# Combining the first expert layer and dispatching the second inside attention's steps, with heads spread through DRAM and packed loads

## The chip, the cores and the metric

The kernel runs on one core of one Trainium2 chip. TensorE (PE in the profile) does matrix products and transposes into PSUM; VectorE (DVE), ScalarE (ACT) and GpSimd (POOL) work on what stands there or in SBUF; SyncE (SP) and POOL issue the DMAs. The metric is the device time of one execution in microseconds. The kernel before has a median of 851.75 us over three runs, from 846.43 to 854.3.

## The reference

`x` is 8 sequences of 256 tokens with 128 features each, all in float32. Six blocks follow one another, each added to `x`:

```python
x = x + 0.5 * ffn(layernorm(x))          # mixture of experts, weights L0_ffn
x = x + attn(layernorm(x))               # 16 heads of 8
x = x + 0.5 * ffn(layernorm(x))          # the same mixture of experts again
x = x + 0.5 * channel_mix(layernorm(x))  # token shift, relu^2, sigmoid gate
x = x + gated_conv(layernorm(x))         # a long convolution by a Fourier transform
x = x + 0.5 * channel_mix(layernorm(x))

def ffn(s):                               # 2048 tokens
    h = rmsnorm(s @ W_in.T, in_norm_w)
    logits = h @ Wr.T                     # 8 experts
    idx = top_k(logits + expert_bias, 2)
    gates = softmax(logits at idx)        # 0 elsewhere
    out = sum over e of gates[:, e] * rmsnorm((silu(h @ Wg[e].T) * (h @ Wu[e].T)) @ Wd[e].T, enorm_w[e])
    return rmsnorm(out, out_norm_w) @ W_out.T
```

Attention is plain softmax attention within a sequence, with scale 8 ** -0.5.

## The kernel before

**Tiling.** The 2048 tokens are four chunks (`NCH`) of 512, each held as `xs[c]`, 128 partitions x 4 rows (`TPC`) x 128. Two sequences make a chunk. Everything up to the second expert layer stands in a hand-written order: PE, DVE, ACT and SP run their instructions in the order of the program (`manual_schedule`); only POOL's order is chosen by the scheduler.

**Expert layer, `moe_ffn(f, ...)`, f = 0 and 1.** `dispatch(f, c, mp)` gives four steps per chunk: `product` (four transposes of x into PSUM bank "sa", mean and variance on DVE, four products with `win_r`, squares on ACT), `normed` (a root on ACT, the scaled rows `hrow`, the logits), `choice` (13 small DVE operations for the top two, then PE's `prank` and DVE's `at_row`, `pos`, `posi`: the place of each row in its expert's region), and `rows` (eight indirect DMAs on POOL, L433, which scatter the rows to `hs` in DRAM). `stagger` (one step of each chunk in turn) interleaves the four chunks. `table` computes from the counts which expert and which rows each of 23 tiles of 256 rows takes. `experts` runs these tiles: SP fetches rows `hst_f` and the expert's weights `w_f` (832 KB) three tiles ahead, PE does gate, up and down, ACT and DVE the silu and the product, and POOL scatters the results to `y2` in DRAM (L568). `combine(f, c, ...)` has four steps: `fetch` (SP, two rows per token), `add` (a reciprocal root of 8 numbers per partition on POOL, L610, then eight DVE operations), `turned` (four transposes, squares on ACT, another root on POOL, L634) and `out_` (four products with `wout_o`, four DVE additions to x). In stage 0, all four chunks are combined before attention begins; in stage 1 all four are dispatched after attention has ended.

**Start.** About 28 small loads on SP, with the four chunks of x among the first ten, and eight DMAs that fill the row buffer `hs` with zeros (L117), 516 KB each. POOL clears the constant lanes of q, k, v and m meanwhile (L683, L684, L979).

**Attention.** 32 steps s = (sequence b, head group g of four heads), then eight more for what is left over. In step s, PE does `scores(s, 0)`, `turn_top(s - 1)`, `scores(s, 1)`, the step's extras, `weights(s - 1, 0)`, `average(s - 2)`, `weights(s - 1, 1)`; DVE does `qa` for step s - 1 (L799), `top(s, 0)`, the extras, `top(s, 1)` (L787); ACT does the two exponentials (L818) and every other step `keep`. The extras are listed by step: `turn_back`, `turn_heads` and `out_heads` of each sequence at 4b+6 to 4b+9 (`out_heads` adds to x), the parts of the filter's decay at steps 2, 4 and 6, and the projection of chunk c at 8c-7 (`norm_rows`), 8c-5 (`turn_rows`), 8c-4 and 8c-3 (`to_heads` for q and k) and 8c-2 (`values`). Chunk 0's projection stands before step 0. All extras share the PSUM bank "sa", one at a time, with the transposed maxima of `turn_top`. `norm_rows` takes mean and variance on DVE and the rest on POOL (L705 to L709). `to_heads` copies the product to SBUF, and then SP issues 16 DMAs of 16 KB, which spread the heads over partitions (L730).

After the second expert layer come `channel_mix`, `gated_conv` and `channel_mix`; they are scheduled, and not touched.

Of the kernel before, what the change touches and what calls it, by code (L numbers as in the profile page):

```python
# [10 lines left out]
F32 = mybir.dt.float32  # L11
# [5 lines left out]
P = 128  # L17
B, S, D = 8, 256, 128
NCH = 4
# [18 lines left out]
FILL = 8  # L38
# [5 lines left out]
def macaron_kernel(ctx: ExitStack, tc: tile.TileContext, a: dict, out: bass.AP):  # L44
# [42 lines left out]
    def load(name, shape, src=None, eng=None):  # L87
        t = const.tile(shape, F32, tag=name, name=name)
        (eng or nc.sync).dma_start(t, a[name] if src is None else src)
        return t  # L90

    def load_col(name):
        return load(name, [P, 1], a[name].rearrange("(p o) -> p o", o=1))

    load_x(0)
    win = load("win", [P, D])
    inw = load_col("inw")
    wr_t = load("wr_t", [P, E])
    load_x(1)
    eb = load("eb", [P, E], a["eb"].partition_broadcast(P))  # L100
    tabc = load("tabc", [P, 2 * E * E + 2 * NT * E + NT + 2 + 2 * E])
    tri = load("tri", [P, P])
    load_x(2)
    load_x(3)
    tokid = const.tile([P, NCH * TPC, 2], I32, tag="tokid", name="tokid")
    nc.sync.dma_start(tokid, a["tokid"])
# [3 lines left out]
    nc.vector.memset(zero, 0.0)  # L110


    hs = tc.dram_tile([HS_ROWS, ROW], F32, name="hs")
    region = hs[1 : 1 + E * REGION, :].rearrange("(e c p r) w -> e c p (r w)", e=E, c=2, r=8 * FILL)
    for e in range(E):
        some = zero[ts(e, P // E), :].unsqueeze(1).to_broadcast([P // E, 8, FILL * ROW])
        nc.sync.dma_start(region[e, 0].rearrange("p (i w) -> p i w", i=8), some)  # L117

    rpe_in = load("rpe_in", [P, FEAT], a["rpe_in"].partition_broadcast(P), eng=nc.sync)
    rpe_g = load("rpe_g", [P, LAYERS, FEAT], a["rpe_g"].partition_broadcast(P), eng=nc.sync)  # L120
    rpe_b = load("rpe_b", [P, LAYERS, FEAT], a["rpe_b"].partition_broadcast(P), eng=nc.sync)
    rpe_hid = load("rpe_hid", [FEAT, LAYERS, FEAT], a["rpe_hid"].rearrange("l i o -> i l o"), eng=nc.sync)
    rpe_out = load("rpe_out", [FEAT, D], eng=nc.sync)
    decay = load("decay", [P, D], a["decay"].partition_broadcast(P), eng=nc.sync)

    csm = load("csm", [P, 3])
    idx_col, onehot = csm[:, 0:2], csm[:, 2:3]
    onw = load_col("onw")
    wout_t = load("wout_t", [P, D])

    dft = load("dft", [P, 2, 512], a["dft"].rearrange("(i p) f -> p i f", p=P))
    idft = load("idft", [P, 4, S], a["idft"].rearrange("(q p) m -> p q m", p=P))

    wq_t = load("wq_t", [P, D])
    wk_t = load("wk_t", [P, D])
    wv_t = load("wv_t", [P, D])
    wo_t = load("wo_t", [P, D])
    rw_r = load("rw_r", [P, D])
    rw_k = load("rw_k", [P, D])
    rw_v = load("rw_v", [P, D])  # L140
    mu_r = load_col("mu_r")
    mu_k = load_col("mu_k")
    w_uv = load("w_uv", [P, 2 * D])
    w_go = load("w_go", [P, D])

    om_r = const.tile([P, 1], F32, tag="om_r", name="om_r")
    om_k = const.tile([P, 1], F32, tag="om_k", name="om_k")
    for dst, src in ((om_r, mu_r), (om_k, mu_k)):
        nc.vector.tensor_scalar(dst, src, -1.0, 1.0, ALU.mult, ALU.add)
# [170 lines left out]
    o += 2 * NT * E  # L320
    tid = tabc[:, o : o + NT]
    slot = tabc[:, o + NT : o + NT + 2]
    base = tabc[:, o + NT + 2 : o + NT + 2 + E]
    order = tabc[:, o + NT + 2 + E : o + NT + 2 + 2 * E]
# [6 lines left out]
    def dispatch(f, c, mp):  # L331
# [4 lines left out]
        def product():  # L336
# [16 lines left out]
            for t in range(TPC):  # L353
                nc.tensor.matmul(
                    st["pp"][:, t // 2, t % 2, :], xt[:, ts(t, P)], win_r, start=True, stop=True
                )
# [147 lines left out]
    def experts(f, tab, far, y2, mp, pieces):  # L504
# [74 lines left out]
        for t in range(3):  # L579
            fetch(t)  # L580
# [509 lines left out]
```

## Time and profile before

| | us |
|---|---|
| median of three runs (lowest, highest) | 851.75 (846.43, 854.3) |
| the profiled execution, its time | 851.69 |
| its span in the trace | 849.8 |
| start to first gate of stage 0 | 83.6 |
| experts, stage 0 | 83.6 to 217.2 |
| combination of four chunks, projection of chunk 0 | 217 to 292.5 |
| attention from the first `qa` to the last `out_heads` | 292.5 to 500.5 |
| dispatch of four chunks, table, first rows | 500.5 to 565.5 |
| experts, stage 1 | 565.5 to 695 |
| combination, channel mix, convolution, channel mix | 695 to 849.8 |

Mean granted TensorE clock 0.821 of full; PE busy 624.0 us (73%), DVE 393.1 (46%), ACT 260.7 (31%), POOL 251.2 (30%).

How to read it: the busy digits of the time slices and the stretches' table tell where an engine is full and where none is; a timeline line gives start, duration, engine, line of the kernel, operation, what it writes and reads, how often, and in brackets how long the engine had been idle and what ended that. `PEclk` is the granted clock of TensorE, 1.00 or 0.50 here. An average over the span says little, since the stages have different limits.

### The profile page before, as it was taken

What the parts mean: (1) busy time and instruction counts of PE and PEld (TensorE: products, weight loads), DVE (VectorE), ACT (ScalarE), POOL (GpSimd) and SP (SyncE); (2) the same over time, 40 slices, a digit from 0 to 9 for tenths busy, and PEclk for the clock granted to TensorE, in tenths of its full rate; (3) what the DMA queues carried; (4) which work ended last, traced back from release to release, by engine and by line L of the source; (5) the groups of instructions that cost most, each with busy time, mean ns of one, the idle gap of its engine ahead of it and who ended that gap; (6) DMA issues with size and microseconds to landing.
All of it is one profiled execution on the core that took longest, in us unless ns stands there. A gap on an engine that the chain in (4) does not pass through costs nothing. (4 is left out here: it accounts for less than half of the span.)

```text
span 849.8 us, 11683 instructions
## 1 busy us (share of the span) xinstructions
PE 624.0 (73%) x4019; PEld 478.3 (56%) x4019; DVE 393.1 (46%) x1017; ACT 260.7 (31%) x613; POOL 251.2 (30%) x250
## 2 busy tenths in 40 slices
PE   2520999999344599999999965249999963467974
PEld 2520889899232355656556535239999952344563
DVE  4660445444241243645545515614444434784684
ACT  3310232233221152444444443102323321446132
POOL 4276233333332010200200004722333333360353
PEclk9555999999755587999999975559999995598988
DMA  8723656664200001000010000155666603000001
GB/s 165 168 95 119 194 180 199 198 183 135 74 26 10 16 6 20 2 10 18 2 25 1 2 1 31 50 205 159 204 207 195 192 29 101 1 1 0 1 0 50
DMA packets 44619, 69.57 MB, mean 82 GB/s; under 512 B 7883, under 2 KB 34162, under 8 KB 44560
## 3 DMA queue, kind: packets, MB, share of 16 engines
q1 hardware_dynamic: 39568, 60.34, 24.8%
q0 software_dynamic: 4992, 8.48, 2.9%
q8 instruction: 32, 0.52, 0.2%
q14 instruction: 27, 0.22, 0.1%
HBM read 52.96 MB, written 15.58 MB: 81 GB/s over the span
## 5 line engine op out<-in xcount | busy, mean ns | idle before, releaser
L568 POOL DMA_INDIRECT y<-yrow_f,idx_f x92 | 90.1, 980 | 171.8 <-issue 166.2
L433 POOL DMA_INDIRECT hs<-hrow,posi_f x64 | 61.7, 964 | 153.6 <-DVE ri_f L369 108.6
L818 ACT ACTIVATE es<-ps 128x1024 f32<-128x1024 f32 x64 | 65.4, 1024 | 102.4 <-PE ps L810 102.4
L530 PE MATMUL pg_f<-ht_f,w_f 128*128 128x256 f32 x368 | 90.8, 391 | 5.0 <-DMA w_f<-in_wall_dram 5.0
L550 PE MATMUL py_f<-w_f,hg_f 128*128 128x128 f32 x736 | 90.2, 276 | 2.4 <-DVE yrow_f L561 2.4
L787 DVE TENSOR_REDUCE m<-pm 128x4 f32<-128x1024 f32 x64 | 77.2, 1216 | 31.4 <-PE pm L774 31.4
L774 PE MATMUL pm<-k,q 32*128 32x256 f32 x512 | 81.5, 439 | 13.8 <-DMA k<-kc 11.7
L550 PEld LDWEIGHTS py_f<-w_f,hg_f 128*128 128x128 f32 x736 | 88.6, 192 | 4.9 <-DVE yrow_f L561 2.7
L539 PE MATMUL pu_f<-ht_f,w_f 128*128 128x256 f32 x368 | 87.9, 382 | 0.0
L543 DVE TENSOR_TENSOR hg_f<-pu_f,sg_f 128x1024 f32<-128x1024 f32 x46 | 56.4, 1225 | 62.9 <-PE pu_f L539 62.9
L532 ACT ACTIVATE sg_f<-pg_f 128x1024 f32<-128x1024 f32 x46 | 47.1, 1024 | 117.3 <-PE pg_f L530 117.3
L810 PE MATMUL ps<-qa,k 32*128 32x256 f32 x512 | 76.5, 421 | 0.0
L530 PEld LDWEIGHTS pg_f<-ht_f,w_f 128*128 128x128 f32 x368 | 68.7, 197 | 13.7 <-issue 5.8
L539 PEld LDWEIGHTS pu_f<-ht_f,w_f 128*128 128x128 f32 x368 | 67.3, 193 | 7.4
L774 PEld LDWEIGHTS pm<-k,q 32*128 32x128 f32 x512 | 48.2, 204 | 26.0 <-DMA k<-kc 14.2
L560 ACT ACTIVATE ysq_f<-py_f 128x128 f32<-128x128 f32 x92 | 24.6, 273 | 122.9 <-PE py_f L550 117.6
L810 PEld LDWEIGHTS ps<-qa,k 32*128 32x128 f32 x512 | 46.3, 195 | 24.8 <-issue 16.2
L524 DVE TENSOR_SCALAR ht_f<-pht_f,inw 128x256 f32<-128x256 f32 x46 | 22.3, 484 | 67.4 <-PE pht_f L522 67.4
L799 DVE TENSOR_TENSOR qa<-pmt,q 128x256 f32<-128x256 f32 x32 | 13.6, 425 | 85.6 <-PE pmt L793 85.6
L522 PE MATMUL pht_f<-ident,hst_f 128*128 128x128 f32 x92 | 18.7, 287 | 40.6 <-DMA hst_f<-hs 40.6
L561 DVE TENSOR_TENSOR yrow_f<-py_f,w_f 128x256 f32<-128x256 f32 x46 | 19.6, 426 | 53.5 <-ACT ysq_f L560 53.5
L625 PE MATMUL pan_f<-ident,acc_f 128*128 128x128 f32 x32 | 9.4, 448 | 46.4 <-DVE acc_f L616 46.4
(244 smaller groups left out, 927.5 us busy)
## 6 DMA issues: line engine op xcount, KB each, us to landing
w_f<-in_wall_dram SPq DMA_DIRECT2D x46, 832.0 KB
hst_f<-hs SPq DMA_DIRECT2D x46, 129.0 KB
hs<-zero SPq DMA_DIRECT2D x8, 516.0 KB
y_f<-y SPq DMA_DIRECT2D x16, 258.0 KB
y<-yrow_f,idx_f POOLq DMA_INDIRECT x92, 4.5
x<-in_x_dram SPq DMA_DIRECT2D x4, 256.0 KB
hs<-hrow,posi_f POOLq DMA_INDIRECT x64, 2.4
q<-qc SPq DMA_DIRECT2D x64, 16.0 KB
```

The costliest lines, as they stand in the source:

```text
L433: ins = nc.gpsimd.indirect_dma_start(out=hs, out_offset=bass.IndirectOffsetOnAxis(ap=st["posi"][:, t, k : k + 1], axis=0), in_=hrows[c][:, ...
L530: nc.tensor.matmul(pg[:, k, :], w[t][:, ts(k, P)], ht[t], start=True, stop=True)
L532: nc.scalar.activation(sg, pg, AF.Silu)
L539: nc.tensor.matmul(pu[:, k, :], w[t][:, DFF + k * P : DFF + k * P + P], ht[t], start=True, stop=True)
L543: nc.vector.tensor_mul(hg[t], pu, sg)
L550: nc.tensor.matmul(py[:, s, :], hg[t][:, k, ts(s, P)], w[t][:, 2 * DFF + k * D : 2 * DFF + k * D + D], start=(k == 0), stop=(k == NFC - 1),)
L560: nc.scalar.activation(sq[:, s], py[:, s], AF.Square, accum_out=yrow[:, s, D : D + 1])
L568: ins = nc.gpsimd.indirect_dma_start(out=y2, out_offset=bass.IndirectOffsetOnAxis(ap=idx[:, s : s + 1], axis=0), in_=yrow[:, s, :], in_off ...
L774: nc.tensor.matmul(sc[:, jj, i, :], qs[c][r, g, col + i * P : col + (i + 1) * P], ks[c][r, g, col : col + S], start=True, stop=True,)
L787: nc.vector.tensor_reduce(m, sc, AX.X, ALU.max, negate=True)
L810: nc.tensor.matmul(sc[:, jj, i, :], ks[c][r, g, col + i * P : col + (i + 1) * P], tops[s][r, :], start=True, stop=True,)
L818: nc.scalar.activation(es, sc, AF.Exp, scale=scale)
```

## The change

1. *Order.* `moe_ffn` is taken apart. Stage 0's dispatch and experts run as before; `combined` then yields the steps of each chunk's combination (`add` together with the fetch of the chunk after next, `turned`, `out_`). Chunk 0's steps run before attention; chunk c's (c = 1 to 3) are extras of steps 8c-8 to 8c-6. The dispatch of stage 1 for chunk c is extras of steps 8c+14 to 8c+20, so chunks 0 and 1 lie within the 32 steps, chunk 2 has its last five steps after them, and chunk 3 all seven. The loop has 45 steps, not 40.
2. *Dispatch* has seven steps (`turned`, `product` twice, `normed`, `choice`, `places`, `rows`), goes through one bank at a time, and copies the product to SBUF (`u`). For f = 1 the root is POOL's, not ACT's.
3. *Projection*: `norm_rows` normalises on DVE, with only the root on POOL; it stands at 8c-5, `turn_rows` and the first `to_heads` share 8c-4, then 8c-3 and 8c-2. `to_heads` writes q and k of a chunk to DRAM in one DMA of 512 KB and reads them back, spread, in four of 128 KB.
4. *Loads*: five packs in place of the small loads; chunks 2 and 3 of x are loaded behind the zeros, which are written in pieces of half the size (`FILL` 4). ACT does a first Sqrt early. The constant lanes are cleared on POOL beside the first ten expert tiles. The weights of the first three tiles are fetched ahead of their rows; `yrow` has two buffers, not three.

The core of the diff:

```diff
-FILL = 8
+FILL = 4
...
     load_x(0)
+    win, wr_t, inw, eb, tri, slot, base, order, tokid = pack(
+        "pack1", [D, E, 1, E, P, 2, E, E, NCH * TPC * 2]
+    )
     load_x(1)
...
-        nc.sync.dma_start(region[e, 0].rearrange("p (i w) -> p i w", i=8), some)
+        nc.sync.dma_start(region[e, 0].rearrange("p (i w) -> p i w", i=16), some)
+    load_x(2)
+    load_x(3)
...
+        def product(i):
+            pp = bank(f"pin_{n}_{i}", "sa" if f else None)[:, 0 : 2 * (D + E)]
...
+            u = st["u"][:, 2 * i : 2 * i + 2]
+            nc.scalar.copy(u, pp)
...
+            if f == 0:
+                nc.scalar.activation(ri, ri, AF.Sqrt)
+                nc.vector.reciprocal(ri, ri)
+            else:
+                nc.gpsimd.tensor_tensor(ri, ri, mhalf.to_broadcast([P, TPC]), ALU.pow)
...
-        return product, normed, choice, rows
+        return turned, partial(product, 0), partial(product, 1), normed, choice, places, rows
...
         for t in range(3):
-            fetch(t)
+            fetch_weights(t)
+        for t in range(3):
+            fetch_rows(t)
...
-                nc.gpsimd.tensor_scalar(rs, mv[:, :, 1], LN_EPS, None, ALU.add)
+                nc.vector.tensor_scalar(rs, mv[:, :, 1], LN_EPS, None, ALU.add)
                 nc.gpsimd.tensor_tensor(rs, rs, mhalf.to_broadcast([P, TPC]), ALU.pow)
...
-                    nc.gpsimd.tensor_scalar(
+                    nc.vector.tensor_scalar(
...
-                for j in range(4):
-                    for g in range(4):
-                        r = 32 * j + HD * g
-                        nc.sync.dma_start(dst[32 * j : 32 * j + HD, g, :], t[r : r + HD, :])
+                if i == 1:
+                    there = tc.dram_tile([P, 2, CT], F32, name=f"heads{c}")
+                    nc.sync.dma_start(there, qkc[c])
+                    back = there.rearrange("(j g d) i s -> j d i g s", j=4, g=4)
+                    for j in range(4):
+                        nc.sync.dma_start(qks[c % 2][32 * j : 32 * j + HD], back[j])
...
+            for c in range(NCH):
+                project = [
+                    partial(norm_rows, c),
+                    partial(turn_rows, c),
+                    partial(to_heads, c, 0),
+                    partial(to_heads, c, 1),
+                    partial(values, c),
+                ]
+                if c == 0:
+                    for step in (*before[0], *project):
+                        step()
+                else:
+                    for i, step in enumerate(before[c]):
+                        extra[8 * c - 8 + i].append(step)
+                    for i, step in zip((-5, -4, -4, -3, -2), project):
+                        extra[8 * c + i].append(step)
+                for i, step in enumerate(after[c]):
+                    extra[8 * c + 14 + i].append(step)
...
+    def combined(f, gates, y2, gp):
+        chunks = [combine(f, c, gates, y2, gp) for c in range(NCH)]
+        for chunk in chunks[:2]:
+            chunk[0]()
+        ahead = [chunk[0] for chunk in chunks[2:]] + [lambda: None] * 2
+        return [(both(add, fetch), *rest) for fetch, (_, add, *rest) in zip(ahead, chunks)]
...
+            stagger([dispatch(0, c, gp) for c in range(NCH)])
+            gates = run_experts(0, y2s[0], gp, [both(*two) for two in zip(early, idle)])
+            mixed = combined(0, gates, y2s[0], gp)
+            attention(mixed, [dispatch(1, c, gp) for c in range(NCH)])
+            gates = run_experts(1, y2s[1], gp, [])
+            stagger(combined(1, gates, y2s[1], gp))
```

## The prediction

> **What bounds the kernel now.** I read the time slices first, then busy time by stretch, then the order of instructions around each seam, and last the order on VectorE inside attention. From the page, busy tenths in 40 slices of 21.2 us:
>
> ```profile
> PE   2520999999344599999999965249999963467974
> DVE  4660445444241243645545515614444434784684
> POOL 4276233333332010200200004722333333360353
> PEclk9555999999755587999999975559999995598988
> ```
>
> PE is full in the two expert stages and in attention. Between them lie two valleys with half of PE's clock: slices 11-14 (combining stage 0, projecting heads) and 24-26 (dispatch of stage 1). The stretches, columns PE, PEld, DVE, ACT, POOL, granted clock, DMA share, GB/s:
>
> ```profile
> 221.80:257.60 35.80, 13.00 (x48) 10.04 (x48) 13.73 (x61) 7.03 (x36) 10.50 (x8) 0.50 0.23 59
> ...
> 313.94:317.35 3.41, 1.66 (x20) 0.80 (x12) 0.59 (x2) 3.37 (x6) 0.00 (x0) 1.00 0.13 24
> ...
> 441.00:488.00 47.00, 47.00 (x470) 29.05 (x466) 27.11 (x38) 20.07 (x24) 0.00 (x0) 1.00 0.02 4
> 500.50:565.40 64.90, 23.07 (x92) 19.83 (x92) 28.73 (x157) 16.26 (x58) 30.81 (x32) 0.50 0.17 52
> ```
>
> In the valleys no engine is half busy: they are chains of waits. In 441-488 PE is never idle. So work taken out of a valley shortens it fully, and what it costs inside attention is what PE is made to do and to wait for.
>
> **The change part by part.** All sums start from the profiled execution: span 849.8 us, its time 851.69, 1.9 more; the median 851.75 is the same within 0.1 us.
>
> *Start.* The input of chunks 2 and 3 is now queued behind the eight transfers that zero the row buffer. These moved 4.2 MB at some 180 GB/s (stretch 6.0-33.6) and ended near 33.5. The hand order puts `turned(3)` ahead of chunk 0's `normed`, `choice` and `places` on PE, ACT and DVE, so chunk 0's first scatter waits for x3: about 32.7, then some 9.5 us of chain (positions came 10 us apart per chunk, at 27.6 and 37.7, and that round holds the same steps) and 0.9 to the scatter: 43.1 against 36.50. The 32 scatters keep their pace of 1.26 us. Weights fetched before the table's rows save some of the 2.3 us wait for `w_f` ahead of the first gate; I take 1.8. Together +4.8; below, -2 (the wait goes and x3 is early), above, +10 (zeros in pieces of half the size are slower). Clearing constants beside the experts adds some 13 us to POOL in ten tiles of 5.46 us whose scatters take 2 us each, and the output rows lose their third buffer: both are hidden by the 3.4 us that POOL has free per tile; without that cover, 0 to +5. The early Sqrt on ACT costs nothing before the first x lands.
>
> *Before attention.* Here is the seam, in the order of the trace:
>
> ```profile
> 226.47 0.17 DVE L609 TENSOR_SCALAR cf_f<-y_f 128x8 f32<-128x8 f32 x1 [6.37 <-DMA y_f<-y]
> 226.73 1.67 POOL L610 TENSOR_TENSOR cf_f<-cf_f,mhalf 128x8 f32<-128x8 f32 x1 [5.18 <-DVE cf_f L609]
> ...
> 256.44 1.13 DVE L643 SCALAR_TENSOR_TENSOR x<-pout_f,ori_f,x 128x128 f32<-128x128 f32 x4 [1.12 <-POOL ori_f L634]
> ...
> 278.30 10.65 SPq L730 DMA_DIRECT2D k<-kc  x16
> ...
> 292.50 0.42 DVE L799 TENSOR_TENSOR qa<-pmt,q 128x256 f32<-128x256 f32 x1 [0.84 <-PE pmt L793]
> ```
>
> Only chunk 0 is now combined here. Alone, it has x at 235.4 (sums 230.56, transposes, squares and POOL's root to 234.2, 1.1 on DVE) where all four took until 257.57: -22.2. The normalised rows go from POOL's 3.12 us to four of DVE's operations near 0.2 us: -2.3. So `kc` is ready at 245.45, not 269.98. The heads then took 18.3 us (269.98 to the last scores that waited for `k`, at 288.33), 32 issues of some 0.68 us on SP's queue, as the line at 278.30 shows for sixteen. Now one write of 512 KB is followed by four reads of 128 KB: a 258 KB transfer took 3.8 us here (222.68 to 226.47), so write and read are an estimate of 9.5 us. Between 5 (two latencies of 2.3, as `hst_f` shows from 559.77 to 562.07) and 21.7 (five of these transfers in a row plus issues). First scores to the first `qa` took 4.2; `add(1)` stands in step 0 ahead of it, 5 more. 245.45 + 9.5 + 4.2 + 5 = 264.2 against 292.5: **-28.3**. On SP the four reads wait for the write, and behind them stands only a fetch of `y` for chunk 3, which nobody needs until step 16.
>
> *Inside attention.* Three combinations (chunks 1-3) and the dispatches of chunks 0, 1 and the first two steps of chunk 2 move into steps 0-31. VectorE in the steps that already carry the projection of a chunk:
>
> ```profile
> 362.81 0.42 DVE L799 TENSOR_TENSOR qa<-pmt,q 128x256 f32<-128x256 f32 x1 [2.03 <-PE pmt L793]
> ...
> 369.60 0.42 DVE L799 TENSOR_TENSOR qa<-pmt,q 128x256 f32<-128x256 f32 x1 [3.42 <-PE pmt L793]
> ```
>
> From one `qa` to the next is a step. This one takes 6.8 us, the next three (`qa` at 376.37, 383.53, 390.82) 6.8, 7.15 and 7.3, where plain steps take 5.2 to 5.45. An extra that fills the one PSUM bank "sa" and is copied out so costs 1.5 to 2.0 us, 1.75 in the mean. Moved in are 16 such (turned and out of three combinations; turned, two products and places of two dispatches, turned and one product of a third): 16 x 1.75 = 28.0. VectorE has about 2 us free in a plain step (its wait at 362.81). Three `add` steps need 4.1 (226.47 to 230.56, POOL's root inside): 3 x 2.1 = 6.3. `choice` is 13 operations of 0.22, 2.9, and `normed` waits for a root on POOL: 0.9 + 1.2, twice, 4.2. Normalising on DVE: 0.9 x 3 = 2.7. Last, POOL's queue: in its order three scatters of chunk 0 stand ahead of the root that `norm_rows(3)` in step 19 needs; DVE stands in order behind that root, so `top`, then `qa`, then PE wait: 3 x 1.26 and what is left of a root and its handover, 5.1. Sum **+46.3**. Bounds: PE's own part is 13.00 / 4 at half clock per combination and 23.07 / 4 per dispatch, 1.6 and 2.9 at the full one: 3 x 1.6 + 2.5 x 2.9 = 12.1 if every wait hides; above, 55, as chunks did in the valleys (7.4 us and 10 us).
>
> *Clock.* One wait in attention shows the second price. In 313.94-317.35 VectorE waits 4.8 us for ACT's table loads and PE works 1.66 of 3.41 us; then the clock is 0.50 until 331.0, 13.6 us, about 6.8 us lost. Windows of 0.78 busy kept it. I expect two new such holes, at step 19 and at one crowded step near 17: **+13.7**; none to five: 0 to +34.
>
> [...]
>
> *After attention.* Before, x of chunk 3 was final at 500.07, four chunks of dispatch followed at 10 us, POOL's last of 32 scatters began at 557.24, the first gate at 565.46:
>
> ```profile
> 557.24 0.95 POOL L433 DMA_INDIRECT hs<-hrow,posi_f  x1 [0.30 <-issue]
> ...
> 565.46 0.77 PE L530 MATMUL pg_f<-ht_f,w_f 128*128 128x256 f32 x1 [2.70 <-DMA w_f<-in_wall_dram]
> ```
>
> Now one chunk is left. Its x is 7 us later within the tail (chunk 2's last five dispatch steps lie there), 14.4 us from x to positions (17.0 before, from 500.07 to 517.05, less a table load of 1.3 and 1.6 in which `lg` waited for `hrow` and that now comes first, and a little for the second bank), 3 us behind chunk 2's eight scatters on POOL, 0.9, 7 x 1.26, then 8.2 - 2.7 to the gate: 539.8. **-25.3** (-32 with a clean tail, -15 if the scatters of two chunks queue fully, 10.1 more).
>
> Sum: 849.8 + 4.8 - 28.3 + 46.3 + 13.7 - 25.3 = 861.0; with 1.9, 862.9. Experts, second combination and the rest are unchanged.
>
> **The rivals.** *The steps stay full.* PE pays only its own part and short waits, say 20 of the range's 12.1 to 55, and no new hole appears: 849.8 + 4.8 - 28.3 + 20 - 25.3 = 821.0, 823 in time, up to 843. For it: VectorE is busy 27.11 of 47 us; against it: a single "sa" bank, whose users took 1.75 us each. It decides where the loop grows by less than 40 without holes. *Waits, but no holes:* 847.3, 849 in time: no change. *Holes everywhere:* four or five, slow heads: 27 more, near 885. *That the dispatch doesn't hide:* if POOL's scatters hold up each root, the tail gains only 15: 873.
>
> **How the numbers follow.** Slower as summed, with more holes or a poor tail among it, 0.52; no change 0.15; full steps 0.33. A measurement of this kernel tells about 1% from no change. The likeliest case's own range is 853 to 886; to leave out no more than 2 in 10, it goes down to 822.
>
> **What would show it.** First scatter near 43; first `qa` near 264; steps 16-23 near 8.6 us where they took 6.2; clock 0.50 in one or two stretches within attention; gate 40 us after the last `out_heads`, not 65. Attention growing by under 40 us at full clock would prove the sum wrong, so would heads over 20 us.

## The result and the profile after

The kernel after takes **886.23 us** (median, 884.69 to 887.76), the kernel before on the same chip 853.02 us: ratio 1.0403, 95% interval 1.0341 to 1.0464. It is slower by 4%, and 23 us slower than forecast. The profiled execution took 886.61 us, its span is 884.8 us, the mean granted clock 0.804 (before 0.821).

The time slices of the page of after, one slice being 22.1 us:

```profile
PE   2330999999248898888789997339999944558774
DVE  1371455444215444445534552414444425783664
POOL 0076266333201001001400210522333333542242
PEclk8555899999755698797779695559999985589887
```

The two valleys have become short (slices 11-12 and 25-27), as meant. But attention (slices 13-24), a solid row of 9 before (slices 15-23), is now mostly 8s, and the clock row under it is broken. The same by stage, in us between marks of the traces (first gate matmul, first and last `qa`, first and last line of the combination):

| | before | after | predicted change | measured change |
|---|---|---|---|---|
| start to first gate | 83.58 | 91.17 | +4.8 | +7.6 |
| first gate to first `qa` | 208.92 | 181.54 | -28.3 | -27.4 |
| first `qa` to last `qa` | 195.79 | 258.63 | +60.0 (46.3 + 13.7) | +62.8 |
| last `qa` to first gate of stage 1 | 77.17 | 58.73 | -25.3 | -18.4 |
| experts and combination, stage 1 | 168.71 | 169.35 | 0 | +0.6 |
| channel mixes and convolution | 115.63 | 125.38 | 0 | +9.8 |

The valleys gave back 45.8 us; attention took 62.8. The stretches of after as the trace gives them (the loop, the tail, the rest; columns PE, PEld, DVE, ACT, POOL, granted clock, DMA share, GB/s):

```profile
272.71:531.34 258.63, 225.96 (x1770) 135.51 (x1770) 121.96 (x278) 97.45 (x163) 27.02 (x26) 0.83 0.09 19
531.34:590.07 58.73, 23.38 (x109) 15.28 (x109) 17.68 (x87) 12.81 (x32) 17.56 (x18) 0.52 0.21 67
759.42:884.80 125.38, 83.95 (x360) 58.54 (x360) 78.28 (x124) 41.87 (x72) 45.04 (x32) 0.83 0.03 9
```

Before, the loop had the clock at 0.94. The clock's intervals say why: it was at half for 24.9 us of the loop before, and for 87.1 us, in eight spells and the loop's start, after. A score product (L812) took 670 ns in the mean at half clock (302 to 308.6 us of after) and 400 at the full one (320 to 332), 1.7 times as long; were it twice, (87.1 - 24.9) / 2 = 31 of the 62.8 us would be clock, so 31 is an estimate from above. In the traces of before and after every change of the clock within the span lies on a grid of 3.413 us, to within 0.001 us; one cell of it is called a window here, and a hole is a time in which PE stands idle within a step. One spell opens where the projection normalises chunk 1 (timeline of after):

```profile
292.10 1.01 POOL L704 TENSOR_TENSOR ars<-ars,mhalf 128x4 f32<-128x4 f32 x1 [13.30 <-DVE ars L703]
293.14 1.12 DVE L707 TENSOR_SCALAR xn_a<-x,amv,ars 128x128 f32<-128x128 f32 x4 [1.12 <-POOL ars L704]
294.17 1.22 DVE L789 TENSOR_REDUCE m<-pm 128x4 f32<-128x1024 f32 x1
295.45 0.69 PE L795 MATMUL pmt<-ident,m 128*128 128x128 f32 x2 [2.15 <-DVE m L789]
296.17 0.42 DVE L801 TENSOR_TENSOR qa<-pmt,qk 128x256 f32<-128x256 f32 x1 [0.78 <-PE pmt L795]
...
308.50 0.42 DVE L801 TENSOR_TENSOR qa<-pmt,qk 128x256 f32<-128x256 f32 x1 [8.62 <-PE pmt L795]
```

DVE waits for a root on POOL, normalises, and only then reduces `m`; PE stands for 2.15 us. PE is busy for 1.75 us of the 3.41 us of this window:

```profile
291.55:294.96 3.41, 1.75 (x28) 0.93 (x18) 2.25 (x10) 2.35 (x4) 1.01 (x1) 1.00 0.02 5
```

From 294.96 to 308.61 the clock is 0.50, and the next step, full of work, takes 12.33 us. The hole itself cost some 2 us, the half clock after it some five by estimate (the steps with `to_heads` of chunks 2 and 3 took 6.8 to 7.2 us before).

But not every spell has such a hole ahead of it. Here are two windows of after with nearly the same PE work and the same longest gap, 0.77 us ahead of the products of `places`; the first was followed by full clock, the second by half:

```profile
424.66:428.08 3.42, 2.65 (x24) 1.56 (x20) 2.38 (x7) 1.02 (x1) 0.00 (x0) 1.00 0.00 0
496.35:499.76 3.41, 2.64 (x23) 1.80 (x19) 2.65 (x8) 1.02 (x1) 0.00 (x0) 1.00 0.00 0
```

The windows ahead of the eight spells had 1.07 to 2.64 us of PE work, five of them 2.21 or less. So holes and half clock go together in most cases, but no share of work and no length of a gap that decides is shown.

In what follows a ratio is made of undisturbed executions alone, so it can differ from the quotient of two medians, and of `c_after` and `v1`, whose profiles caught a disturbed execution, no stage times are used.

### The profile page after: what moved, and what is told of

Its sections match the earlier page's. It is cut to its first block, busy times and chain, and to the rows that moved or that the text cites. A ratio compares the mean times of both kernels' runs of the same rounds, so it can differ in the third digit from the quotient of the medians.

```text
span 884.8 us, 11427 instructions
## 1 busy us (share of the span) xinstructions
PE 647.9 (73%) x4019; PEld 484.6 (55%) x4019; DVE 393.4 (44%) x1033; ACT 265.3 (30%) x624; POOL 243.1 (27%) x234
## 3 DMA queue, kind: packets, MB, share of 16 engines
q1 hardware_dynamic: 36336, 62.43, 24.9%
## 5 line engine op out<-in xcount | busy, mean ns | idle before, releaser
L776 PE MATMUL pm<-qk 32*128 32x256 f32 x512 | 86.9, 463 | 11.6 <-DMA qk<-heads 7.6
L812 PE MATMUL ps<-qa,qk 32*128 32x256 f32 x512 | 87.9, 478 | 0.0
L812 PEld LDWEIGHTS ps<-qa,qk 32*128 32x128 f32 x512 | 52.1, 224 | 31.2 <-issue 22.5
L776 PEld LDWEIGHTS pm<-qk 32*128 32x128 f32 x512 | 51.5, 217 | 24.8 <-issue 12.4
L801 DVE TENSOR_TENSOR qa<-pmt,qk 128x256 f32<-128x256 f32 x32 | 13.6, 424 | 101.5 <-PE pmt L795 101.5
L516 DVE TENSOR_SCALAR ht_f<-pht_f,pack 128x256 f32<-128x256 f32 x46 | 22.2, 484 | 66.1 <-PE pht_f L514 66.1
L605 POOL TENSOR_TENSOR cf_f<-cf_f,mhalf 128x8 f32<-128x8 f32 x8 | 13.1, 1642 | 109.7 <-DVE cf_f L604 109.7
```

The source lines that it names most:

```text
L776: nc.tensor.matmul(sc[:, jj, i, :], qs[c][r, g, col + i * P : col + (i + 1) * P], ks[c][r, g, col : col + S], start=True, stop=True,)
L812: nc.tensor.matmul(sc[:, jj, i, :], ks[c][r, g, col + i * P : col + (i + 1) * P], tops[s][r, :], start=True, stop=True,)
```

## The experiments

The times of before differ between the chips (852 to 861 us), so each kernel is judged by its ratio to before on the same chip. Stage times come from one profile each.

**The unchanged pair, for scale.** `c_after` is the changed kernel, `c_before` the kernel before, each run once more on the chips of the experiments. No edit.

> The changed kernel itself, beside the others on one chip, for the four runs so far were on a chip where engines waited up to 8 us at a time for signals already given while POOL scattered. Expected 3.5 to 5.5% above the kernel before; the loop from first to last qa 258 to 283 us, stretches as recorded otherwise.

> The kernel before itself, with a profile beside the others on one chip, so that its stretches can be set against those of the runs so far. Expected: ratio 1; first gate between 84 and 92 us, loop 195 to 197, from last qa to first gate of stage 1 77 to 80, behind the last combination 116.

Measured: `c_after` 901.57 us, ratio 1.0475 (1.0421 to 1.0529). `c_before` 861.86 us, ratio 0.9995 (0.9959 to 1.0032), its last stretch 118.10 us. So the changed kernel's loss is 4.0 to 4.8%, by chip.

**The rest: bank counters.** The convolution's code is unchanged, but the PSUM counters reach it at other values, and the scheduler orders VectorE differently there.

```diff
+    turn.update(bank=0, pair=1)
     channel_mix(0)
```

> The changed kernel takes 10.4 us longer than the kernel before from the first gate of stage 1 to the end, nearly all of it behind the second combination, in code that the diff does not touch. This run is the changed kernel with one line more: ahead of the first channel mix the two counters that hand out PSUM banks in turn are set to what they were there in the kernel before (0 and 1; the change leaves 3 and 2, for its dispatch draws eight single banks and no pair). VectorE's order in the convolution is then that of the kernel before again. Theory order (banks in turn decide where the scheduler puts the second channel mix among the convolution): last gate to end 285 us, not 294.7, time 876 to 879. Rival clock phase (the clock's free windows fall differently, whatever the order): 294 us again, time 885 to 888.

Measured: the last stretch 117.31 us instead of 125.38; the whole 902.47 us, ratio 1.0465 (1.04 to 1.0531), not distinguishable from `c_after`. VectorE in this stretch, first in after, then in `e_banks`:

```profile
828.35 0.69 DVE L153 TENSOR_REDUCE mean_c<-x 128x4 f32<-128x512 f32 x1
...
831.20 0.69 DVE L170 TENSOR_REDUCE lnrs_c<-sq_ln_c 128x4 f32<-128x512 f32 x1 [0.76 <-ACT sq_ln_c L169]
831.80 0.68 DVE L962 TENSOR_TENSOR tmp<-pvf,tf 128x512 f32<-128x512 f32 x1
```

```profile
845.29 0.68 DVE L964 TENSOR_TENSOR tmp<-pvf,tf 128x512 f32<-128x512 f32 x1
845.88 0.68 DVE L965 TENSOR_TENSOR tmp<-pvf,tf 128x512 f32<-128x512 f32 x1
...
853.13 0.69 DVE L153 TENSOR_REDUCE mean_c<-x 128x4 f32<-128x512 f32 x1
```

In after, operations of the second channel mix (`mean_c`, `lnrs_c`) stand ahead of the convolution's `tmp`, which then starts without VectorE having been idle, and PE later stands 3.18 us for what is made of it (PE in after, then in `e_banks`):

```profile
838.79 7.39 PE L973 MATMUL pgo<-pack,prod 128*128 128x256 f32 x20 [3.18 <-POOL prod L966]
```

```profile
846.78 4.51 PE L973 MATMUL pgo<-pack,prod 128*128 128x256 f32 x18 [0.15 <-POOL prod L966]
```

With the counters of before the two products come first. The 8 us are shown for the stretch (a second time in `e_edges`), and over the profiles it takes 121.5 to 125.4 us with the counters as changed and 115.6 to 119.3 with the old ones, so the order is worth 2 to 10 us by profile. The 8 us don't show in this kernel's total: its start (102.85 us) and its loop (282.52 us) were longer than in after by more, in the same profile. In its start:

```profile
71.41 0.19 DVE L412 TENSOR_TENSOR at_row_f<-prank_f,pack 128x32 f32<-128x32 f32 x1 [7.54 <-remote]
71.66 0.59 PE L440 MATMUL pcnt<-macc,ones 128*128 128x8 f32 x2 [8.41 <-issue]
```

The operand `prank_f` was ready at 63.25, yet VectorE and PE both stood still to 71.4 while POOL scattered. The first profile of after has no such stall.

**Filling holes in the changed kernel.** `average` is the matmul group of a step; repeating it gives PE work in the hole.

```diff
+HOLES = (3, 9, 11, 17, 19, 25, 27)
...
+                if s in HOLES:
+                    average(s - 2)
+                    average(s - 2)
```

> In the changed kernel the clock is at half for 87 us of the 258.6 us from the first to the last qa, in the kernel before for 25 of 195.8. Here PE repeats, at the end of steps 3, 9, 11, 17, 19, 25 and 27, the average of two steps ago twice (16 products, some 2.1 us at the full clock, same result in the same bank): it adds PE work where it stood idle. Theory clock (half of the loop's growth is half clock, which sets in where a window is less than about half busy): at least four of the spells within the loop go, the loop takes 230 to 245 us in spite of 15 us more work, time 862 to 876. Rival waits (the steps are long because of what VectorE and POOL do, and the clock only follows): the loop stays within 4 us of 258.6 or grows, by up to 15; time 884 to 902.

Measured: 896.37 us, ratio 1.0417 (1.0362 to 1.0472); loop 266.58 us. The expected 230 to 245 us were missed. Half clock in the loop was 76.4 us, against 113.8 and 139.5 in `e_pool_order` and `e_banks` on the same chip, but other kernels with the same steps had loops of 265.9 (`e_norm_pool`) to 282.5 us (`e_banks`), and three steps became worse (15.25, 16.14 and 17.08 us for 9.59, 13.10 and 10.40): there was less half clock, but the loop did not become clearly shorter.

**POOL's queue at step 19.** The cast of the positions moves one step later, so that all eight scatters stand behind the root of `norm_rows(3)`.

```diff
-            st["posi"] = small.tile([P, TPC, 2], I32, tag="posi", name=f"posi_{n}")
-            nc.vector.tensor_copy(st["posi"], pos)
+            st["pos"] = pos
 
         def rows():
+            st["posi"] = small.tile([P, TPC, 2], I32, tag="posi", name=f"posi_{n}")
+            nc.vector.tensor_copy(st["posi"], st["pos"])
```

> In step 19 of the changed kernel three scatters of chunk 0 stand ahead of the root of norm_rows(3) on POOL; VectorE waited 4.21 us for it, PE 5.33 us, and the clock then was at half for 17 us. Here the last small operation of places (the cast of the row positions) stands at the head of rows instead, one step later, so that the eight scatters follow the root; nothing else moves. Theory queue (those three scatters make the hole, and the hole the slow clock): step 19 takes 8 to 9 us, not 13.1, step 20 8 to 9, not 13.5, time 875 to 880. Rival (VectorE's own work in that step makes it long): step 19 shorter by no more than the 3.8 us of three scatters, step 20 unchanged, time 882 to 887.

Measured: 903.15 us, ratio 1.0491 (1.0443 to 1.0539): no gain. What the queue does is as foreseen: in after the root waits behind scatters and VectorE behind it,

```profile
433.53 0.96 POOL L422 DMA_INDIRECT hs<-hrow,posi_f  x1 [0.30 <-ACT es L820]
434.51 1.05 POOL L704 TENSOR_TENSOR ars<-ars,mhalf 128x4 f32<-128x4 f32 x1
435.60 1.28 DVE L707 TENSOR_SCALAR xn_a<-x,amv,ars 128x128 f32<-128x128 f32 x4 [4.21 <-POOL ars L704]
...
437.90 0.69 PE L795 MATMUL pmt<-ident,m 128*128 128x128 f32 x2 [5.33 <-DVE m L789]
```

and in `e_pool_order` PE's wait there fell from 5.33 to 0.42 us and step 19 from 13.10 to 9.93 us. But half clock came all the same, at 438.23, and stayed for 30.7 us: steps 20 and 21 took 13.99 and 11.39 us, 13.48 and 7.09 in after. The window ahead of it has no hole, only a gap of 0.77 us at the products of `places`:

```profile
434.82:438.23 3.41, 2.64 (x24) 2.04 (x22) 2.43 (x9) 0.00 (x0) 0.00 (x0) 1.00 0.02 5
```

So the theory that this hole makes the slow clock failed; what started it here stays open.

**Both moves undone, the rest of the change kept.**

```diff
-            end = last + 6 + len(after[0])
+            end = last + 8
...
-            attention(mixed, [dispatch(1, c, gp) for c in range(NCH)])
+            stagger(mixed)
+            attention([()] * NCH, [[] for c in range(NCH)])
+            stagger([dispatch(1, c, gp) for c in range(NCH)])
```

> The changed kernel with its combination of all four chunks again ahead of attention, and its dispatch of four chunks again behind it; loads, heads through DRAM, projection steps, bank use and the rest as changed. Theory interleaving (moving the two into the steps costs 63 us in the loop and saves some 20 and 25 outside, so loses on its own): loop 205 to 212 us, combination and dispatch outside as in the kernel before, start 7.6 us and end 10 us later as in the changed kernel, heads faster by 4: time 858 to 872. Rival (the other parts of the change, heads and projection, cost as much in the steps as the interleaving): time 880 or more.

Measured: 905.32 us, ratio 1.0513 (1.0465 to 1.0561), 33 us over the top of the expectation, the largest miss of the study. The loop, with nothing of stage 0 or 1 in it, still takes 20.7 us more than before:

```profile
310.75:527.29 216.54, 203.40 (x1682) 121.44 (x1682) 102.30 (x170) 82.42 (x100) 3.02 (x3) 0.84 0.08 16
```

The same 1682 matmuls as before, at a clock of 0.84 instead of 0.94: 67.4 us at half clock against 24.9, half of the difference, again an estimate from above, being 21.3 us, as much as the whole growth. Steps 4, 6, 12 and 20 take 12.3, 13.1, 13.2 and 12.0 us (12 and 20 took 6.77 before). So the projection as changed costs by itself 20.7 us in the loop, where I had put 2.7. The rest of the miss lies outside: 103.25 us to the first gate, 12 more than in the profile of after, and 86.88 from the last `qa` to the gate of stage 1, where the kernel before took 77.17.

**One move each.** `e_dispatch_out` keeps the combination in the steps and has the dispatch after attention; `e_combine_out` the reverse.

```diff
-            attention(mixed, [dispatch(1, c, gp) for c in range(NCH)])
+            attention(mixed, [[] for c in range(NCH)])
+            stagger([dispatch(1, c, gp) for c in range(NCH)])
```

```diff
+            stagger(mixed)
+            mixed = [()] * NCH
             attention(mixed, [dispatch(1, c, gp) for c in range(NCH)])
```

> The changed kernel with the dispatch of stage 1 again behind attention, all four chunks; combination stays in the steps. Theory (what is moved into the steps pays: the combination costs about 15 us in the loop for 26 outside, the dispatch about 25 for 28): loop 225 to 240, from last qa to first gate of stage 1 84 to 88 us, time within 8 us of the changed kernel beside it. Rival, as forecast (16 users of the one bank at 1.75 us and the holes are the loss, so that the dispatch in the steps loses more than it saves): 10 to 20 us faster than the changed kernel.

> The changed kernel with all four chunks combined ahead of attention; the dispatch stays in the steps. The loop was 216.5 us with both out, 230.3 with the combination alone in the steps, 278 to 282 with both on this chip (258.6 in the first profile). Theory (each piece pays with its own holes; the dispatch, with its scatters on POOL ahead of the roots and its four users of the one bank, is the dear one): loop 250 to 270, from last qa to gate 57 to 60, to the first qa 207; time 905 to 920, slower than the changed kernel. Rival (the two are dear only together): loop 225 to 240, time 885 to 895.

Measured: `e_dispatch_out` 898.89 us, spread over 888.8 to 909.5, too wide for a ratio; its two lower executions (888.8 and 892.4) lie below every one of `c_after` on the same chip (from 900.06). `e_combine_out` 899.05 us, ratio 1.0546 (1.0486 to 1.0606). By stages, against `e_both_out`: the combination adds 13.8 us to the loop (230.34 against 216.54) and takes 25.2 away ahead of it (182.26 against 207.50); the dispatch adds 36.0 to the loop (252.57 against 216.54) and takes 28.2 from the tail (58.64 against 86.87). By these stage times the combination's move pays and the dispatch's doesn't. They are of one profile each, on three chips, and loops with the same steps differ by up to 24 us, so the 7.8 us lost by the dispatch are not settled by them: `e_combine_out` and `e_both_out` have ratios whose intervals overlap.

**The edges.** Chunks 2 and 3 of x ahead of the zeros, stage 1's rows ahead of the weights, and the bank counters of `e_banks`.

```diff
     load_x(1)
+    load_x(2)
+    load_x(3)
...
-    load_x(2)
-    load_x(3)
     (tabc,) = pack("pack2", [2 * E * E + 2 * NT * E + NT])
...
         for t in range(3):
-            fetch_weights(t)
+            if f:
+                fetch_rows(t)
+            else:
+                fetch_weights(t)
...
+    turn.update(bank=0, pair=1)
     channel_mix(0)
```

> The changed kernel with three repairs that lie in three different stretches: chunks 2 and 3 of x loaded ahead of the zeros again; for stage 1 the rows of the first tiles fetched ahead of their weights again; bank counters set to the old values before the first channel mix. Expected of each in its own stretch, against the changed kernel: first scatter 6 to 9 us earlier and with it the first gate (rival: the zeros end last anyway, under 3 us); from last scatter to first gate of stage 1 8 us, not 10 (the last scatters no longer share the DMA engines with 2.5 MB of weights; rival: the gate then waits for its weights instead, no gain); behind the last gate 8 us less. Sum 15 to 20 us; rival 8.

Measured: 883.52 us, ratio 1.0261 (1.0197 to 1.0326), 18 us under `c_after` on the same chip. First scatter in after and in `e_edges`:

```profile
31.63 0.87 DVE L329 BATCH_NORM_STATS2 ast_f<-x 128x6 f32<-128x128 f32 x4 [24.71 <-DMA x<-in_x_dram]
...
45.85 1.21 POOL L422 DMA_INDIRECT hs<-hrow,posi_f  x1 [44.49 <-DVE eq_f L379]
```

```profile
32.80 1.21 POOL L422 DMA_INDIRECT hs<-hrow,posi_f  x1 [31.43 <-DMA pack<-in_pack_dram]
```

VectorE stood 24.71 us for chunk 2 of x, and chunk 0's `normed` and places stood behind it. With x early the first gate comes at 78.18 instead of 89.8 to 103.3 us, the range of the profiles with the new dispatch and late x. It takes both: `e_out_old` and `e_norm_dve` (below) have x just as late, but in the old four steps chunk 0's places come ahead of chunk 2, VectorE waits 7.67 and 7.86 us, and the first scatter starts at 31.81 and 31.73. The last stretch fell to 117.34 us, as in `e_banks`. The third edit was worth nothing: the gate then waits for weights instead of rows (`e_edges`, last line of the tail):

```profile
595.38 3.44 PE L522 MATMUL pg_f<-ht_f,w_f 128*128 128x256 f32 x8 [5.28 <-DMA w_f<-in_wall_dram]
```

**Engine or place?** `e_norm_pool` gives the normalising back to POOL in the same steps. `e_out_old` has both moves undone, the old four-step dispatch, POOL's normalising, and the old gap of two steps between it and the transposes; what is left of the change is, in the main, the packs, the loads' order and the heads through DRAM. `e_norm_dve` is `e_out_old` with VectorE normalising.

The first diff is all of `e_norm_pool` and a part of `e_out_old`, the second the rest of `e_out_old` beside what `e_both_out` has.

```diff
-                nc.vector.tensor_scalar(rs, mv[:, :, 1], LN_EPS, None, ALU.add)
+                nc.gpsimd.tensor_scalar(rs, mv[:, :, 1], LN_EPS, None, ALU.add)
...
-                    nc.vector.tensor_scalar(
+                    nc.gpsimd.tensor_scalar(
```

```diff
-        return turned, partial(product, 0), partial(product, 1), normed, choice, places, rows
+        return product, normed, choice, rows
...
-                    for i, step in zip((-5, -4, -4, -3, -2), project):
+                    for i, step in zip((-7, -5, -4, -3, -2), project):
```

> The changed kernel with the normalising of norm_rows on POOL again, as in the kernel before (variance plus epsilon, root and four rows of xn); the steps are where the change put them. With combination and dispatch out of the steps, the loop was 216.5 us, still 20.7 above the kernel before, and the growth stood at steps 3 to 6, 11 to 12 and 19 to 20: the projection. Theory (VectorE, in order, waits in norm_rows for POOL's root, top is late, PE runs dry for some 2 us in a window, and the next step, which now holds turn_rows and to_heads together, runs at half clock): without that wait the loop takes 235 to 248 us where the changed kernel beside it takes 258 to 283, a gain of 14 to 25. Rival (the wait moves to turn_rows, one step later, for POOL's normalising takes 4.4 us): gain under 6 us.

> Combination before and dispatch behind attention, as in the run with both out, and on top of that three things as in the kernel before: norm_rows on POOL at step 8c-7 with turn_rows, q, k and values at 8c-5, -4, -3, -2; the dispatch in its four old steps (pair of banks, root on ACT); and by the latter the old bank counts. What is left of the change are the loads and the heads through DRAM. Theory (the projection's new place and engine cost 20 us in the loop, the dispatch's new form 9.7 behind it, the order behind the experts 8): loop 196 to 200 us, from last qa to first gate 77 to 79, behind the last combination 116; time 30 to 38 below the run with both out, 866 to 876. Rival (heads through DRAM disturb the loop): loop 205 or more.

> The run with everything out and old (857.5 us, loop 193.6), with one thing as changed: norm_rows normalises on VectorE; its steps are the old ones. Theory engine (VectorE waits 1.1 us for POOL's root ahead of top, then 1.1 us of its own, PE runs dry and the clock falls): a spell of half clock behind steps 1, 9 and 17, loop 203 to 215. Rival place (turn_rows and to_heads in one step, right behind norm_rows, make the loss): loop 193 to 198.

Measured: `e_norm_pool` 899.92 us, ratio 1.0466 (1.0408 to 1.0525), as `c_after`: the wait moves one step on, where PE stands 3.41 us for ACT's copy of the transposes in step 4 and 1.31 us for POOL in step 20. `e_out_old` 857.51 us, ratio 0.997 (0.9937 to 1.0004), loop 193.61: heads through DRAM, packs and loads by themselves are worth 0 to 0.6%. `e_norm_dve` 848.81 us, ratio 0.9945 (0.9908 to 0.9982), loop 197.42. So the engine costs 3.8 us, close to my 2.7; they stand in the steps with `norm_rows` (1, 9 and 17: 0.56, 1.56 and 1.84 us longer). That the place makes the rest of the 20.7 follows by elimination; no run moved the place alone. (That `e_norm_dve` as a whole is no slower comes from its start: first gate at 77.85 us, 85.14 in `e_out_old` with the same code there.) The same operations stand in `e_norm_dve`'s step 9, and there PE's gap is 1.49 us, the window 2.47 busy of 3.41, and the clock stays at 1.00:

```profile
346.02:349.43 3.41, 2.47 (x32) 1.43 (x24) 2.25 (x11) 2.39 (x3) 1.01 (x1) 1.00 0.01 2
```

In `e_both_out`, at step 11, the gap is 1.94 and the window 1.69 of 3.41, and half clock follows:

```profile
391.84:395.25 3.41, 1.69 (x24) 0.96 (x16) 2.27 (x6) 2.00 (x3) 1.01 (x1) 1.00 0.00 0
```

**The hole of the kernel before, filled.** Two repeated matmul groups in step 4 of before.

```diff
+HOLES = (4,)
...
+                if s in HOLES:
+                    average(s - 2)
+                    average(s - 2)
```

> The kernel before with one addition: at the end of step 4 PE repeats the average of two steps ago twice (16 products, some 2.1 us, same result in the same bank), where it waited 2.1 us for ACT's table loads and the clock then fell to half for 13.6 us. Theory (a window of 3.41 us less than about half busy brings four windows at half clock): that spell is gone, steps 4 and 5 take 7 to 9 us, not 10.5 and 10.1, time 4 to 8 us below the kernel before. Rival (no change: PE was only waiting for ACT, or the window falls elsewhere): within 2 us of it, or slower.

Measured: 856.56 us, ratio 0.9957 (0.9931 to 0.9983). VectorE still waits 4.80 us for ACT, but PE now works through it, and the clock is 1.00 from 307 to 498 us. The loop takes 189.6 us, 192.6 in `c_before` on the same chip:

```profile
319.16 2.23 PE L829 MATMUL po<-es,v 128*32 128x256 f32 x32
320.38 0.43 DVE L284 TENSOR_TENSOR filt<-filt,dec 128x256 f32<-128x256 f32 x1 [4.80 <-ACT dec L283]
```

This is the cleanest evidence on the clock: work added, time gone, though only 0.4%.

**Versions.** `v1`: x early, old dispatch after attention, combination in the steps, POOL's normalising at (-6, -5, -4, -3, -2). `v2` is `v1` with the filler in steps 4, 8, 10 and 16. `v3` is `e_out_old` with x early and the filler in step 4, so without the combination in the steps.

The first diff is of `v1` against after, beside the old dispatch and POOL's normalising as in `e_out_old` and x as in `e_edges`, the second of `v2` against `v1`.

```diff
-                    for i, step in zip((-5, -4, -4, -3, -2), project):
+                    for i, step in zip((-6, -5, -4, -3, -2), project):
...
-            attention(mixed, [dispatch(1, c, gp) for c in range(NCH)])
+            attention(mixed, [[] for c in range(NCH)])
+            stagger([dispatch(1, c, gp) for c in range(NCH)])
```

```diff
+HOLES = (4, 8, 10, 16)
```

> What the runs so far point to: combination in the steps and heads through DRAM as changed; dispatch in its old form behind attention; norm_rows on POOL at step 8c-6 (behind out_), turn_rows, q, k and values at 8c-5, -4, -3, -2; chunks 2 and 3 of x ahead of the zeros. Theory: first gate 78 to 81, to the first qa 182 to 185, loop 214 to 222, to the gate of stage 1 77 to 79, rest 116: 838 to 850, below the kernel before by 1 to 2.5%. Rival (the combination's root on POOL and eight VectorE operations make holes of their own): loop 226 to 232, 850 to 860, no gain.

> The version with the combination in the steps (loop 223.3 us) with PE's repeats of the average (2.1 us each) at the end of steps 4, 8, 10 and 16, ahead of the windows in which its clock fell (299.95, 337.5, 354.6 and 395.5). Theory (41 us at half clock in the loop are 10 to 20 us lost): at least two of the four spells go, loop 204 to 215, time 838 to 850, 1.5 to 3% below the kernel before. Rival (the holes only move on): loop 220 or more.

> Loads and heads through DRAM as changed, everything else in its old place (857.5 us), with the repeats at step 4 and chunks 2 and 3 of x ahead of the zeros. Theory: 3 to 5 us from the clock, start unchanged: 851 to 856. Against it stands the version with the combination in the steps: theory, that one is faster by 5 to 15 once its clock holds; rival, this one is as fast, and the combination's place is worth nothing.

Measured: `v1` 857.75 us, ratio 0.9879 (0.9802 to 0.9956). **`v2` 838.45 us, ratio 0.9832 (0.9782 to 0.9882)**, faster than both kernels. `v3` 841.03 us, ratio 0.9883 (0.9838 to 0.9929). `v2`'s loop holds the clock from 279.84 to 484.64 us:

```profile
260.61:473.42 212.81, 201.89 (x1846) 122.30 (x1846) 106.30 (x189) 87.02 (x127) 19.52 (x23) 0.95 0.09 18
```

Against `v3` the loop with the combination in the steps, three more fillers and the normalising one step later is 23.0 us longer (212.81 against 189.80), and 28.7 are saved ahead of it: 2.6 us in the medians, with intervals that overlap. So that the combination's place is worth something is not shown.

## Why the prediction was wrong

The direction held, the size didn't: forecast 11 us slower, measured 34.9 in the profiled pair. The misses add up to the distance: start +2.8, before attention +0.9, loop +2.8, after attention +6.9, experts to the end +10.4; 861.0 + 23.8 = 884.8, the span.

*"Experts, second combination and the rest are unchanged": the step that failed most.* This term stood at 0 and measured +10.4, 9.8 of it in the last stretch, though no line of that was touched. I compared code, not the order of instructions; the counters that pick PSUM banks carry over from stage to stage, and `e_banks` and `e_edges` show some 8 us for it.

*After attention.* The last `out_heads` came 22.6 us after the last `qa`, 11.8 before: +10.8 against the 7 I took, since chunk 2's dispatch steps and the clock of the drain (0.50 from 533.89 us to the gate) share it. From there it took 36.1 us to the gate. My terms give 32.6 (the 40 under "What would show it" counts from the old last `out_heads`; they also add up to -25.7, not -25.3). The term that was too small is the last one: 5.5 us from the last scatter to the gate, measured 9.9. Stage 1's weights now go out first, and the fetch of the rows goes out late (timeline of after):

```profile
575.76 2.70 SPq L502 DMA_DIRECT2D w_f<-in_wall_dram  x3
580.13 0.96 POOL L422 DMA_INDIRECT hs<-hrow,posi_f  x1 [0.30 <-issue]
586.45 3.90 SPq L508 DMA_DIRECT2D hst_f<-hs  x4
590.07 1.22 PE L522 MATMUL pg_f<-ht_f,w_f 128*128 128x256 f32 x2 [0.58 <-DVE ht_f L516]
```

6.3 us lie between the last scatter and the fetch that needs it, 2.5 before. In the other profiles too this is 4.3 to 6.4 us where the weights go first and 2.3 to 3.5 where the rows do, 2.3 in `e_edges`. So the delay goes with the order, but the reverse gains nothing either: in `e_edges` the gate then waits for the weights, 10.5 us after the last scatter.

*Start.* First scatter at 45.85, forecast 43.1. The mechanism (late x behind the zeros) was right and `e_edges` shows it. In the detail it is chunk 2 that stands ahead of chunk 0's `normed`, not chunk 3; its wait ended at 31.63, and the chain from there to the scatter took 14.2 us, not 10.4. That zeros in pieces of half the size are slower, the +10 of the range, no run shows: between 10 and 30 us, while they were written, the DMAs moved 178 GB/s in after and 169 in before.

*Before attention.* Right: -27.4 against -28.3. The sum is right partly by luck. The heads' round trip through DRAM was too short by 4.6 us: the write was issued at 253.42, the last scores that waited for what came back ran at 267.56, 14.1 us against my 9.5 (18.3 before). From there to the first `qa` it took 5.15 us, not 4.2 + 5.

```profile
253.42 0.33 SPq L729 DMA_DIRECT2D heads<-qkc  x1
256.06 2.95 SPq L732 DMA_DIRECT2D qk<-heads  x4
267.56 2.10 PE L776 MATMUL pm<-qk 32*128 32x256 f32 x14 [0.56 <-DMA qk<-heads]
```

*The loop: right sum by luck, wrong make-up.* I had 46.3 of waits and 13.7 of clock, two holes; measured are eight spells, up to 31 of clock, and the other half waits. The step that failed is "I expect two new such holes". I counted holes where queues collide (step 19, confirmed: 13.10 us, though `e_pool_order` has half clock there without the hole) and not where VectorE waits for a root in a step that is already full; in normalising alone I saw 2.7 us of VectorE and overlooked that the place would drop the clock: 20.7 by `e_both_out`. For the combination I had 6 x 1.75 + 6.3 = 16.8; `e_dispatch_out` shows 13.8, and `v2` against `v3` 23.0 with three fillers in it. For the dispatch I had 10 x 1.75 + 4.2 + 5.1 = 26.8 and a hole (the 2.9 of `choice` is named there but not in the 46.3), and `e_combine_out` shows 36.0. Steps 16-23 took 9.8 us in the mean, forecast 8.6. These parts sum to over 62.8; they come from other chips, where the loop of the same steps took 266 to 282 us. Why it varies so is open.

*Gaps and the clock.* Before, half clock set in at 317.36 us, in a PE gap of 2.08 us (315.60 to 317.68). In the runs it followed gaps of 1.94 us (`e_both_out`) and 2.15 us (after), and in after even windows whose longest gap was 0.77 to 1.29 us. So half clock after gaps of some 2 us is shown again; neither a length of gap nor a share of work is shown as the mark.

*The rivals.* "The steps stay full" fell with the slices. "That the dispatch doesn't hide" was half right: it hides, but by the stage times it loses in the steps (36.0) more than it gains in the tail (28.2). "Holes everywhere, near 885" was the nearest to what happened, partly for other reasons (its own 27 us more give 890 in time, not 885).

## What to carry to other kernels

Moving a stage's steps into a loop whose engine is full can cost more inside than it saves outside (here 62.8 us against 45.8), once PE stands and its clock falls (0.94 to 0.83 in the loop), so look at each step that gets an extra for a new wait of VectorE on POOL or ACT, keep a step between producer and consumer, and try spare matmuls where a hole stays. Compare the order of instructions over the whole program, not only where lines changed: counters that rotate buffers carry a local change to its far end, here some 8 us of the last stretch (`e_banks`). A reordered load can hold up every chunk when a hand order makes the first chunk stand behind a later one, as in after, where VectorE stood 24.71 us for chunk 2 of x.

## What the runs showed of the hardware

- In the traces of before and after the granted clock is 1.00 or 0.50, and every change within the span lies on a grid of 3.413 us; in `v2` the stretch at full clock from 279.84 to 484.64 us is 60 of these. Windows with 1.66 (before, 313.94 to 317.35), 1.69 (`e_both_out`, 391.84 to 395.25) and 1.75 us of PE work (after, 291.55 to 294.96) were followed by half clock, but so were some with 2.46 to 2.64 (after, 277.89 to 281.31 and 496.35 to 499.76), while others with 2.19 (after, 332.51 to 335.92) and 2.47 (`e_norm_dve`, 346.02 to 349.43) were not; what decides is open. Half clock lasted 2 to 5 windows (6.8 to 17.1 us) in the loop of after. It did not always end with the first window in which PE was full; five full ones in a row stayed at half in `e_both_out`:

```profile
337.23:354.29 17.06, 17.06 (x96) 8.32 (x96) 3.13 (x5) 4.87 (x7) 0.00 (x0) 0.50 0.15 43
```

- Work without use was faster than waiting: 32 matmuls more in step 4 took 0.4% off the kernel before (`e_before_fill`, ratio 0.9957).
- While POOL ran indirect scatters in `e_banks`, one every 1.26 us, VectorE stood 7.54 us and PE 8.41 us up to 71.4 us ("remote" and "issue" in the timeline), though `prank_f` had been ready at 63.25. The profiles of before and after have no wait of VectorE put down to "remote". The cause is open.
